# Cross attentions of a decoder block: context channels split 128 and 64, keys ahead of values

## The chip, the cores and the metric

The kernel runs on one core of a Trainium2 chip. A core has TensorE for matrix products (PE in the profile, PEld its weight loads), VectorE (DVE), ScalarE (ACT), GpSimd (POOL) and SyncE (SP), which here only issues transfers. Matmuls write to PSUM, which has eight banks of 512 float32 values per partition; the kernel's tiles `mm` and `one` are one bank, `sc` and `pair` two. The metric is the device time of one execution in microseconds, lower is better.

## The reference

Six sublayers in a row, each `x = layernorm(x + f(x))`, all float32, on `x` of 8 batches of 256 tokens of 256 channels: a gated convolution, a cross attention, a routed expert layer, a self attention with rotary position, a second cross attention, and a masked attention over all tokens. The two cross attentions have the same form and each its own weights:

```python
q = (x @ Wq).reshape(B, Nq, h, dh)          # h = 16 heads of dh = 64
k = (context @ Wk).reshape(B, Nk, h, dh)    # 77 context rows per batch, 192 channels
v = (context @ Wv).reshape(B, Nk, h, dh)
scores = jnp.einsum('bqhd,bkhd->bhqk', q, k) * scale
attn = jax.nn.softmax(scores, axis=-1)
out = jnp.einsum('bhqk,bkhd->bqhd', attn, v).reshape(B, Nq, h * dh)
return out @ Wo + bo
```

## The kernel before

The sublayers follow one another, and the end of each (its `tail`, a list of pieces) is issued inside the start of the next. In the convolution (`mamba`) the work goes by four stripes of 512 tokens. For a stripe, `state` and `steps` (L249) make products on TensorE; ScalarE takes the absolute value (L257), the exponential (L258) and then, in `gated`, the logarithm (L263); VectorE makes `y` of it (L265 to L273, the first of these reading the PSUM bank of `steps`). ScalarE holds one set of function tables at a time; a change of set shows as ACT_TABLE_LOAD. `outputs` (L282), a layer norm and `turn_out` (transposes at L88, a copy at L93) end a stripe.

In `cross`, the keys are never multiplied with queries directly. `keys(q, part)` (L427) makes the transposed keys of two batches for eight heads; `weighted_keys(q, g)` (L445) multiplies them with Wq into `M`, two heads side by side on the upper and lower 64 rows of the array; `scores(u)` (L464) multiplies tokens with `M`. The same is done for values: `values(c, g)` (L370) makes the transposed values of a chunk of 128 of the 616 context rows (five chunks, the last of 104), `weighted_values(c, g)` (L389) multiplies them with Wo, two heads side by side, into `U`, which goes to DRAM (L402) and comes back per batch as `Ub` (L411, L415). A unit `u` is eight heads of one batch; there are 16. In unit `u` the kernel issues `scores(u + 1)` with its softmax (maximum and subtraction on VectorE, L471 and L473; exponential on ScalarE, L477; sums on VectorE, division on GpSimd, L484), `outputs(u - 1)` (L509), then pieces of keys and values by two small tables (`more`, and a branch on `k`), then `turn(u)`, the transposes of the probabilities (L493). Copies out of PSUM go to ScalarE and VectorE in turn (`evac`, L74 and L76). The pieces needed before unit -1 are the list `first`; `places` says behind which of them each piece of the previous `tail` goes. Each engine works through its own queue in order.

The context has 192 channels, more than the 128 rows of the array. Before, they are two halves of 96 rows: 16 matmuls for eight pairs of heads. The weights come as 96 x 2 x 1024.

The second cross attention is followed by `signs.add`, whose chain over ScalarE, VectorE and GpSimd (L1284 to L1298) runs in its units. Its first pieces stand behind the last block of the rotary attention, whose norm is on GpSimd (L116), behind a power of 128x16 (L1272).

Of the kernel before, what the change touches and what calls it, by code (L numbers as in the profile page):

```python
# [10 lines left out]
F32 = mybir.dt.float32  # L11
# [7 lines left out]
P = 128  # L19
# [3 lines left out]
NCTX, DCTX = 77, 192  # L23
EPS = 1e-5
# [25 lines left out]
def decoder_kernel(ctx: ExitStack, tc: tile.TileContext, a: dict, out: bass.AP):  # L50
    nc = tc.nc
# [91 lines left out]
    def mamba(xs, W, cv, my, close):  # L143
# [4 lines left out]
        with pool_of(tc, name="m1", bufs=1) as m1, pool_of(  # L148
            tc, name="m2", bufs=2
        ) as m2, pool_of(tc, name="mps", bufs=2, space=PSUM) as mps:  # L150
            done, xc, sz, y, bc = [], {}, {}, {}, {}

# [5 lines left out]
            def one():  # L158
                return mps.tile([P, 512], F32, tag="one", name="one")
# [76 lines left out]
            def state_sums(s, bc_p):  # L236
                ps = one()
                last = nc.tensor.matmul(ps, ones[:16, :], bc_p[:16, :], start=True, stop=True)
                bc[s] = m1.tile([P, 512], F32, tag="bc", name="bc")
                nc.scalar.copy(bc[s], ps)  # L240
                return last
# [48 lines left out]
            def turn_out(s, half, ps):  # L290
                n_s, nT_s = done[s]
                transposed(ps, n_s[:, half * 2 : half * 2 + 2, :], nT_s, half)
# [3 lines left out]
            for s in range(4):  # L296
# [8 lines left out]
                if s > 1:  # L305
                    with tc.issue_after(last.ins):
                        for half in range(2):
                            turn_out(s - 2, half, one())
# [19 lines left out]
    def cross(xs, W, bias, ctxT, at_unit, after, tail):  # L328
# [10 lines left out]
        with ExitStack() as st:  # L339
# [7 lines left out]
            def mm():  # L347
                return cps.tile([P, 512], F32, tag="mm", name="mm")

            def pair():  # L350
                return cps.tile([P, 2, 512], F32, tag="sc", name="sc", bufs=3)
# [6 lines left out]
            def span(c):  # L358
                return c * P, min((c + 1) * P, NB * NCTX)

            def values(c, g):

                lo, hi = span(c)
                if g == 0:
                    VTs[c] = c1.tile([P, 8, P], F32, tag="VT", name="VT")
                ps = mm()
                for i in range(4):
                    hp = g * 4 + i
                    for kc in range(2):
                        nc.tensor.matmul(  # L370
                            ps[:, i * P : i * P + hi - lo], wv[:, kc, hp * P : (hp + 1) * P],
                            ctxT[:, kc, lo:hi], start=kc == 0, stop=kc == 1,
                        )
                evac(
                    VTs[c][:, g * 4 : g * 4 + 4, : hi - lo],
                    ps.rearrange("p (i n) -> p i n", i=4)[:, :, : hi - lo],
                )
# [41 lines left out]
            def keys(q, part):  # L419

                if part == 0:
                    KTs[q] = c1.tile([P, 8, 2 * NCTX], F32, tag="KT", name="KT")
                ps = pair()
                for i in range(4):
                    hp = part * 4 + i
                    for kc in range(2):
                        nc.tensor.matmul(  # L427
                            ps[:, i // 2, i % 2 * 2 * NCTX : (i % 2 + 1) * 2 * NCTX],
                            wk[:, kc, hp * P : (hp + 1) * P],
                            ctxT[:, kc, q * 2 * NCTX : (q + 1) * 2 * NCTX],  # L430
                            start=kc == 0, stop=kc == 1,
                        )
                nc.scalar.activation(
                    KTs[q][:, part * 4 : part * 4 + 4].rearrange("p (a i) n -> p a (i n)", a=2),
                    ps[:, :, : 4 * NCTX], AF.Copy, scale=0.125,
                )
# [93 lines left out]
            for c in range(NCH):  # L530
                for k in range(4):
                    u = (-2, -2, 1, 4, 8)[c] + k if c != 1 else -1 + k // 2
                    more.setdefault(u if c else -2, []).append(
                        lambda c=c, k=k: (values, weighted_values)[k // 2](c, k % 2)
                    )

            first = more[-2] + [
                lambda k=k: (keys, weighted_keys)[k // 2](0, k % 2) for k in range(4)
            ]
            places = (4, 5, 6, 7, 7, 8, 8)  # L540
# [12 lines left out]
            for u in range(-1, NU + 1):  # L553
# [9 lines left out]
                if 0 <= u and q + 1 < NB // 2:  # L563
                    if k < 2:
                        keys(q + 1, k)
                    else:
                        weighted_keys(q + 1, k - 2)
# [1011 lines left out]
    def cross_weights(pool, i, other=None):  # L1579
        return (  # L1580
            weight(pool, a[f"Wv{i}"], 2, 1024, 96), weight(pool, a[f"Wo{i}"], 8, D),
            weight(pool, a[f"Wk{i}"], 2, 1024, 96), weight(other or pool, a[f"Wq{i}T"], 8, D),
        )


    with ExitStack() as st:
# [4 lines left out]
        ctxT = const.tile([96, 2, NB * NCTX], F32, name="ctxT")  # L1591
# [8 lines left out]
        with pool_of(tc, name="wq", bufs=1) as wq:  # L1600
# [10 lines left out]
            nc.sync.dma_start(out=ctxT, in_=a["ctxT"].rearrange("(k p) n -> p k n", p=96))  # L1611
# [91 lines left out]
def _arrays(i):  # L1703

    def c(v):
        return np.ascontiguousarray(v)

    i = {k: np.asarray(v) for k, v in i.items()}
    consts, rot = _constants()
# [4 lines left out]
        "ctxT": c(i["ctx_768"].reshape(NB * NCTX, DCTX).T),  # L1714
# [8 lines left out]
        **{f"W{n}{l}": c(i[f"L{l}_xattn_W{n}"]) for n in "kvo" for l in (0, 1)},  # L1723
# [45 lines left out]
```

## Time and profile before

| what | value |
|---|---|
| three timed runs | 1440.02, 1442.06, 1445.01 us; median 1442.06 |
| profiled execution | 1440.51 us, its span 1438.7 us |
| TensorE clock granted, mean | 0.995 |
| busy: PE, DVE, ACT, POOL | 1369.4, 846.3, 652.0, 482.3 us |
| first cross attention on TensorE | from 159 to 416 us |
| second cross attention on TensorE | from 933 to 1191 us |

The page gives for each engine its busy time and the number of instructions. A group line has the code line, the engine, the operation, what is written and read, the shape (for a matmul, rows x columns of the weights, then rows x columns of the moving operand), the number of records, the busy time, the mean of one in ns, and the idle time before it with what ended it. A line of the chain of waits has the start, the length, the engine, the tile written, the code line and the number of records. A line of the waits has who waited, for whom, and the total, the number of times and the longest in us.

### The profile page before, as it was taken

What the parts mean: (1) busy time and instruction counts of PE and PEld (TensorE: products, weight loads), DVE (VectorE), ACT (ScalarE), POOL (GpSimd) and SP (SyncE); (2) the same over time, 40 slices, a digit from 0 to 9 for tenths busy, and PEclk for the clock granted to TensorE, in tenths of its full rate; (3) what the DMA queues carried; (4) which work ended last, traced back from release to release, by engine and by line L of the source; (5) the groups of instructions that cost most, each with busy time, mean ns of one, the idle gap of its engine ahead of it and who ended that gap; (6) DMA issues with size and microseconds to landing.
All of it is one profiled execution on the core that took longest, in us unless ns stands there. A gap on an engine that the chain in (4) does not pass through costs nothing.

```text
span 1438.7 us, 21959 instructions
## 1 busy us (share of the span) xinstructions
PE 1369.4 (95%) x7946; PEld 960.7 (67%) x7946; DVE 846.3 (59%) x2306; ACT 652.0 (45%) x1608; POOL 482.3 (34%) x509
## 2 busy tenths in 40 slices
PE   8999899999999999999989999999999999899996
PEld 3455578888866666656556666678878787566554
DVE  3776455465543323324668888745555663787885
ACT  3455433343331022221178787632342323877884
POOL 0100012122200133236336666332434445455541
PEclk9999999999999999999999999999999999999999
DMA  9000023333540022342120000024312210000100
GB/s 256 18 1 0 27 94 104 109 94 109 162 190 0 23 69 85 81 139 66 37 81 2 2 1 1 1 94 130 94 48 82 85 35 9 16 16 23 23 16 16
DMA packets 71679, 87.81 MB, mean 61 GB/s; under 512 B 5588, under 2 KB 66164, under 8 KB 71060
## 3 DMA queue, kind: packets, MB, share of 16 engines
q1 hardware_dynamic: 68164, 77.10, 17.6%
q0 software_dynamic: 3408, 9.31, 2.3%
q8 instruction: 64, 1.05, 0.3%
q14 instruction: 43, 0.35, 0.1%
HBM read 56.87 MB, written 29.52 MB: 60 GB/s over the span
## 4 chain that ended last, share of the span: by engine, by line
PE 78%; DVE 12%; POOL 3%; ACT 3%; issue 3%; DMA 0%; POOLq 0%; SPq 0%; DVEq 0%; ACTq 0%
PE mm L509 9%; PE sc L464 8%; PE mm L765 7%; DVE p L1018 6%; PE mm L828 5%; PE op L1055 4%; PE pair L249 4%; PE pair L178 4%; PE ps_sc L1040 4%; PE ps_sc L1009 4%; PE tr L782 3%; PE sc L427 2%; PE tr L842 2%; PE sc L445 2%; PE sc L493 2%
## 5 line engine op out<-in xcount | busy, mean ns | idle before, releaser
L1025 ACT ACTIVATE p<-p,nmx 128x256 f32<-128x256 f32 x512 | 252.9, 495 | 63.7 <-DVE nmx L1018 63.6
L484 POOL TENSOR_TENSOR p<-p,sm 128x616 f32<-128x616 f32 x60 | 72.6, 1215 | 247.3 <-DVE sm L481 217.0
L509 PE MATMUL mm<-Ub,pT 128*128 128x256 f32 (+1 forms) x640 | 144.6, 379 | 0.5 <-ACT pT L74 0.4
L464 PE MATMUL sc<-M,xT_s 128*128 128x308 f32 x512 | 139.6, 423 | 0.8 <-ACT pT L74 0.8
L1040 PE MATMUL ps_sc<-ident,p 128*128 128x128 f32 x1024 | 132.2, 276 | 7.6 <-DVE nmx L1018 3.7
L1040 PEld LDWEIGHTS ps_sc<-ident,p 128*128 128x128 f32 x1024 | 113.5, 141 | 34.4 <-issue 13.3
L509 PEld LDWEIGHTS mm<-Ub,pT 128*128 128x128 f32 (+1 forms) x640 | 120.8, 190 | 20.0 <-ACT pT L74 0.9
L765 PE MATMUL mm<-xT_s,w 128*128 128x512 f32 x256 | 114.9, 601 | 4.0 <-DVE h L771 3.2
L464 PEld LDWEIGHTS sc<-M,xT_s 128*128 128x128 f32 x512 | 94.0, 188 | 33.3 <-ACT pT L74 1.5
L477 ACT ACTIVATE p<-p 128x616 f32<-128x616 f32 x64 | 45.8, 716 | 149.9 <-DVE p L473 128.5
L1018 DVE CUSTOM_DVE_ANT_0 p<-ps_sc,term 128x256 f32<-128x256 f32 x256 | 90.7, 419 | 27.6 <-PE ps_sc L1009 27.5
L1018 DVE CUSTOM_DVE_ANT_0 p<-ps_sc,zero 128x256 f32<-128x256 f32 x256 | 90.7, 420 | 27.3 <-PE ps_sc L1009 25.7
L1025 ACT ACTIVATION_READ_ACCUMULATOR p<-p,nmx 128x1 f32 x512 | 95.8, 187 | 0.0
L765 PEld LDWEIGHTS mm<-xT_s,w 128*128 128x128 f32 x256 | 48.3, 192 | 59.0 <-issue 53.9
L802 POOL DMA_INDIRECT xb<-xd,token x39 | 37.2, 954 | 147.3 <-PE tr L809 81.1
L471 DVE TENSOR_REDUCE nmx<-sc 128x8 f32<-128x616 f32 x64 | 51.1, 798 | 54.3 <-PE sc L464 54.2
L1043 DVE COPY pT<-ps_sc 128x1024 f32<-128x1024 f32 x64 | 77.6, 1213 | 2.8 <-PE ps_sc L1040 2.8
L1043 ACT COPY pT<-ps_sc 128x1024 f32<-128x1024 f32 x64 | 63.7, 996 | 28.8 <-PE ps_sc L1040 28.7
L828 PE MATMUL mm<-wE,xbT 128*128 x156 | 73.5, 593 | 0.3 <-ACT xbT L814 0.3
L769 ACT ACTIVATE g<-mm 128x512 f32<-128x512 f32 x32 | 19.1, 597 | 104.3 <-PE mm L765 98.7
L113 POOL TENSOR_SCALAR rstd<-mv 128x2 f32<-128x2 f32 x48 | 10.7, 224 | 159.3 <-DVE mv L111 158.8
L480 DVE TENSOR_REDUCE sm<-p 128x8 f32<-128x616 f32 x64 | 50.5, 790 | 22.6 <-ACT p L477 21.9
(291 smaller groups left out, 2663.6 us busy)
## 6 DMA issues: line engine op xcount, KB each, us to landing
Ub<-ud SPq DMA_DIRECT2D x32, 512.0 KB
ud<-U SPq DMA_DIRECT2D x16, 616.0 KB
wE<-in_wE SPq DMA_DIRECT2D x4, 1536.0 KB
yd<-y SPq DMA_DIRECT2D x39, 128.0 KB
Ub<-ud SPq DMA_DIRECT2D x32, 104.0 KB
ud<-U SPq DMA_DIRECT2D x4, 608.0 KB
x_s<-in_x SPq DMA_DIRECT2D x8, 256.0 KB
w<-in_Wo SPq DMA_DIRECT2D x2, 1024.0 KB
```

What stands on the lines that cost most here:

```text
L178: last = nc.tensor.matmul(ps[:, i, :], w_in[:, kc, c * P : (c + 1) * P], xT_s[:, kc, :], start=kc == 0, stop=kc == 1,)
L249: last = nc.tensor.matmul(ps[:, i, :], w_dt[:, kc, c * P : (c + 1) * P], xc[s][kc // 2][:, kc % 2, :], start=kc == 0, stop=kc == 3,)
L464: nc.tensor.matmul(sc[:, a, : 4 * NCTX], xT_b[:, kc, j * P : (j + 1) * P], M[:, a * 4 : a * 4 + 4, kc, at : at + NCTX], start=kc == 0, sto ...
L484: engine.tensor_tensor(pv, pv, bcast(sm, 2, [P, 8, NCTX]), ALU.mult)
L509: nc.tensor.matmul(o[:, j * D : (j + 1) * D], pT[:n, c, j * P : (j + 1) * P],  Us[b][:n, g, c], start=g == 0 and j == 0 and c == 0, stop=g ...
L765: nc.tensor.matmul(ps, w[:, kc, cols], xT_s[:, kc, :], start=kc == 0, stop=kc == 1)
L828: nc.tensor.matmul(ps, xT[:, kc, :], column(j, kc * 512, 512), start=kc == 0, stop=kc == 1)
L1009: self.last_score = nc.tensor.matmul(scs[s // 2][:, s % 2, :], self.queries(b, c, s, qb), self.keys(b, c, s), start=True, stop=True, tile_ ...
L1018: self.last = nc.vector.tensor_tensor_reduce(out=p[:, h, :], in0=s4[:, h, :], in1=self.term(b, qb), scale=-1.0, scalar=3.0e38, op0=ALU.add ...
L1025: nc.scalar.activation(p[:, h, :], p[:, h, :], AF.Exp, bias=nmx[:, qb, n : n + 1], scale=-1.0, accum_out=sums[:, qb, n : n + 1],)
L1040: nc.tensor.transpose(tr[:, at : at + P], p[:, h, kb * P : (kb + 1) * P], ident)
L1043: (nc.scalar.copy if j else nc.vector.tensor_copy)(self.pT[b, c, j][:, :, :, qb * P : (qb + 1) * P], tr.rearrange("p (h k t) -> p h k t", ...
```

## The change

The context channels are split 128 and 64. The rest of 64 rows is put twice into `ctxT`, on partitions 0 to 63 and 64 to 127, and the rest of the weights is laid out with one pair of heads on the upper 64 partitions and the next on the lower ones. A new function `from_context` makes keys or values of all 16 heads at once: eight matmuls of 128 rows, then eight of 64 rows, two beside each other, each into its own bank of a pair. It uses the two-bank tiles for values too. The first pieces of `cross` have the order keys, values, weighted keys, weighted values. In the units, all keys of a quarter go into one unit, all values of a chunk into one, and the weighted values of chunks 2 to 4 move a unit earlier. In the convolution an exponential of one column is issued behind the copy of `bc`, and the two copies of `turn_out` in the last stripe go to VectorE.

```diff
+            warm = m1.tile([P, 1], F32, name="warm")
+            nc.gpsimd.memset(warm, 0.0)
...
-                nc.scalar.copy(bc[s], ps)
+                with tc.issue_after(nc.scalar.copy(bc[s], ps).ins):
+                    nc.scalar.activation(warm, warm, AF.Exp)
...
-                            turn_out(s - 2, half, one())
+                            turn_out(s - 2, half, one(), nc.vector.tensor_copy if s == 3 else None)
...
+            def from_context(w, lo, hi, copies, dst):
+                n, pss = hi - lo, [pair(), pair()]
+                for g in range(2):
+                    for a in range(2):
+                        for i in range(2):
+                            hp = g * 4 + a * 2 + i
+                            nc.tensor.matmul(
+                                pss[g][:, i, a * n : (a + 1) * n], w[:, 0, hp * P : (hp + 1) * P],
+                                ctxT[:, 0, lo:hi], start=a == 0, stop=False,
+                            )
+                for g in range(2):
+                    for a in range(2):
+                        for i in range(2):
+                            rest, k = DHEADS + (g * 2 + a) * P, slice(i * 64, (i + 1) * 64)
+                            nc.tensor.matmul(
+                                pss[g][:, i, a * n : (a + 1) * n], w[k, 0, rest : rest + P],
+                                ctxT[k, 1, lo:hi], start=False, stop=a == 1,
+                                tile_position=(i * 64, 0),
+                            )
+                    copies[g](
+                        dst[:, g * 4 : g * 4 + 4, :n].rearrange("p (a i) n -> p i a n", a=2),
+                        pss[g][:, :, : 2 * n].rearrange("p i (a n) -> p i a n", a=2),
+                    )
+            def values(c):
+                VT = VTs[c] = c1.tile([P, 8, P], F32, tag="VT", name="VT")
+                second = nc.scalar.copy if c == 0 else nc.vector.tensor_copy
+                from_context(wv, *span(c), (nc.scalar.copy, second), VT)
...
+            def keys(q):
+                KT = KTs[q] = c1.tile([P, 8, 2 * NCTX], F32, tag="KT", name="KT")
+                def scaled(dst, src):
+                    nc.scalar.activation(dst, src, AF.Copy, scale=0.125)
+                from_context(wk, q * 2 * NCTX, (q + 1) * 2 * NCTX, (scaled, scaled), KT)
...
-            for c in range(NCH):
-                for k in range(4):
-                    u = (-2, -2, 1, 4, 8)[c] + k if c != 1 else -1 + k // 2
-                    more.setdefault(u if c else -2, []).append(
-                        lambda c=c, k=k: (values, weighted_values)[k // 2](c, k % 2)
-                    )
-            first = more[-2] + [
-                lambda k=k: (keys, weighted_keys)[k // 2](0, k % 2) for k in range(4)
+            for c in range(1, NCH):
+                for k in range(3):
+                    u = (-1, 1, 4, 8)[c - 1] + (k if c > 1 else k // 2)
+                    more.setdefault(u, []).append(
+                        lambda c=c, k=k: weighted_values(c, k - 1) if k else values(c)
+                    )
+            first = [
+                lambda: keys(0), lambda: values(0),
+                lambda: weighted_keys(0, 0), lambda: weighted_keys(0, 1),
+                lambda: weighted_values(0, 0), lambda: weighted_values(0, 1),
             ]
-            places = (4, 5, 6, 7, 7, 8, 8)
+            places = (1, 1, 4, 5, 5, 6, 6)
...
-                    if k < 2:
-                        keys(q + 1, k)
-                    else:
+                    if k == 0:
+                        keys(q + 1)
+                    elif k > 1:
                         weighted_keys(q + 1, k - 2)
...
-            weight(pool, a[f"Wv{i}"], 2, 1024, 96), weight(pool, a[f"Wo{i}"], 8, D),
-            weight(pool, a[f"Wk{i}"], 2, 1024, 96), weight(other or pool, a[f"Wq{i}T"], 8, D),
+            weight(pool, a[f"Wv{i}"], 1, 1536), weight(pool, a[f"Wo{i}"], 8, D),
+            weight(pool, a[f"Wk{i}"], 1, 1536), weight(other or pool, a[f"Wq{i}T"], 8, D),
...
-        ctxT = const.tile([96, 2, NB * NCTX], F32, name="ctxT")
+        ctxT = const.tile([P, 2, NB * NCTX], F32, name="ctxT")
...
+    def two_rests(w):
+        rest = w[P:].reshape(DCTX - P, 4, 2, P).transpose(2, 0, 1, 3).reshape(P, 4 * P)
+        return c(np.concatenate([w[:P], rest], 1))
...
+        "ctxT": c(np.concatenate([ctxT, ctxT[P:]])),
```

## The prediction

> **What bounds the kernel now.** I read the page first, then the chain of waits in order of time over both cross attentions, then the groups by form, the waits by stage, and the timelines around the two starts.
>
> ```profile
> span 1438.7 us, 21959 instructions
> PE 1369.4 (95%) x7946; PEld 960.7 (67%) x7946; DVE 846.3 (59%) x2306; ACT 652.0 (45%) x1608; POOL 482.3 (34%) x509
> PE 78%; DVE 12%; POOL 3%; ACT 3%; issue 3%; DMA 0%; POOLq 0%; SPq 0%; DVEq 0%; ACTq 0%
> ```
>
> TensorE is busy 95% of the span and makes 78% of the chain that ended last. What matters is whether that holds where the edit works. In the chain of waits, a stretch of the first cross attention and a `weighted_keys` from another unit:
>
> ```profile
> 234.44 2.30 PE sc L445 x32
> ...
> 323.07 2.09 PE sc L427 x16
> 325.17 1.76 PE mm L370 x16
> 326.93 1.09 PE sc L493 x10
> 328.02 4.15 PE sc L464 x16
> ```
>
> Piece follows piece without a gap. From 200 to 392 us the waits of TensorE add up to 0.8 us. So a microsecond of keys (L427) or values (L370) is a microsecond of the end. A float32 matmul of the code makes two records, so x16 is eight matmuls. By form:
>
> ```profile
> L445 PE MATMUL sc<-KT,w 64*128 64x154 f32 x512 | 37.9, 298 | 0.0
> L427 PE MATMUL sc<-ctxT,w 96*128 96x154 f32 x256 | 36.3, 295 | 0.0
> L370 PE MATMUL mm<-ctxT,w 96*128 96x128 f32 x256 | 31.4, 278 | 2.4 <-ACT xT_s L93 2.4
> L370 PE MATMUL mm<-ctxT,w 96*128 96x104 f32 x64 | 7.7, 274 | 0.0
> ```
>
> L445 is the row to look at: 512 records with 64 rows cost as much as 256 of the same 154 columns with 96 rows (L427). Two half-array matmuls on different rows run side by side: 0.072 us a record against 0.131. And 104 columns of L370 cost what 128 cost (1.76 us per sixteen in the chain), so full-row records have a floor near 0.11 us whatever their columns.
>
> Only the starts have gaps: the waits of 155 to 200 us, then of 930 to 950 us.
>
> ```profile
> PE sc L389 <- DVE VT L76: 2.5, 1, 2.5
> PE mm L370 <- ACT xT_s L93: 2.4, 3, 0.9
> PE sc L389 <- ACT VT L74: 1.6, 1, 1.6
> ...
> PE sc L389 <- DVE VT L76: 2.8, 1, 2.8
> ```
>
> **Part 1: 128 and 64 rows in place of 96 and 96.** Keys of two batches were two groups of L427, 4.19 us. Now eight full-row matmuls (one such group, 2.10) and eight half-row ones, four pairs: half of L445's x32, 1.15. Where the array goes from full to half rows or back the chain shows about 0.1 us (L427 takes 2.19 before L389, 2.10 elsewhere; L370 takes 1.89 after L445 or L389, 1.77 elsewhere); I add 0.1, as before had some of these changes too. 3.35 us, 0.85 saved, eight times: 6.8 us.
>
> A chunk of values was 3.6 us (1.77 or 1.89, twice). Now 1.77 full-row, and eight half-row matmuls of 128 columns, which the trace does not have. Below: L445's rate scaled by columns, 1.15 x 128/154 = 0.95. Above: L445 unscaled, 1.15; far above, the full-row floor, 1.77, if the loads of a pair do not overlap. I take 1.0, as L445 has the same rows and weight shape. With the change 2.87, about 0.7 saved, ten times: 7.0 us. Part 1: 13.8 us, with 12 and 15 as near ends, and 6.1 if loads do not overlap.
>
> [...]
>
> **Part 2: keys first, in the first cross attention.** I walk the new order with old durations, on the old clock. TensorE ends the last transposes (L88) at 159.9. The first key matmul takes the banks of those transposes, whose copies the edit puts on VectorE behind `gated`, which ends at 160.97; two copies (0.6 each) free the banks at 162.25: a wait of 2.35, where L370 waited 0.7. Keys to 165.6. Values wait for the L265 that reads the last step's bank; it needs Ln. Here the table counts:
>
> ```profile
> 159.21 1.02 ACT L257 ACTIVATE e<-pair 128x1024 f32<-128x1024 f32 x1 [3.04 <-PE pair L249]
> 160.72 1.28 ACT L258 ACT_TABLE_LOAD   x1
> 164.86 1.06 ACT L263 ACTIVATE e<-e 128x1024 f32<-128x1024 f32 x1
> ```
>
> The load moves into the 3.04 us that ScalarE idles before L257, with one exponential of 128x1 (not in the trace; between the 0.19 of a 128x1 accumulator read and the 0.58 of a 128x512 copy). 1.9 us at most: covered. Were the cover gone, Ln would come that much later. With two copies (0.48, 0.06 on the path) moved to VectorE too, Ln ends near 163.7, L265 near 164.9: before the keys end. No wait. [...]
>
> Values to 168.5, two transposes, then both `weighted_keys` (4.6 us; eight copies of 0.6 us on ScalarE keep pace), first `weighted_values` 1.85, outputs 3.65, the second, outputs: scores start near 185, against 190.79. Chunk 1 follows with about 1 us of wait (its VT copy queues on ScalarE behind an exponential), and 0.1 later. Waits: 6.5 before (0.7, 0.8, 1.6, 2.5, 0.9), 3.4 after: 3.1 us gained.
>
> **Part 3: keys first, in the second.** No `gated` is in the way and weights are there; L370's 2.8 wait for VT goes. What is late next is the block from the rotary attention:
>
> ```profile
> 936.16 2.93 POOL L1272 TENSOR_TENSOR gss<-gss,nhalf 128x16 f32<-128x16 f32 x1
> 940.23 2.43 POOL L116 TENSOR_SCALAR x_s<-r,mv,rstd 128x256 f32<-128x256 f32 x2
> ```
>
> Its transposes (L88) moved from 946.06 to behind the values, at 940.0, but GpSimd delivers at 942.66, behind L1272. New wait: 2.7 us, with both `weighted_keys` queued behind it on TensorE. Another 0.6 for chunk 1's VT; gone are 2.8 and 0.7 (at 971). Net 0.2.
>
> **Moved at no cost.** `weighted_values` of chunk 0 now come last, so the way of U through DRAM starts later:
>
> ```profile
> 943.29 8.58 SPq L402 DMA_DIRECT2D ud<-U  x4
> 959.49 1.15 SPq L411 DMA_DIRECT2D Ub<-ud  x1
> ```
>
> By the stretches of DMA traffic it falls from 229 to 14 GB/s at 965: 21.7 us from the first issue. The new first issue is near 951, so both halves land by 972.7, and `outputs` 0 needs the first near 975: covered by scores, chunk 1 and keys, with 2 us to spare; in the first cross attention (first issue near 177, need near 210) 11 us. SyncE's queue keeps its order per chunk; the weights for the experts still stand behind the last readers of Wv, Wo and Wk. Later chunks run `weighted_values` a unit earlier, so their loads only gain. Keys and values now hold two pairs of banks: by the order of the changed program each new pair was read one group earlier (a 0.6 to 0.7 us copy against 1.0 of matmuls), so nothing in steady units; bound 0.5 us each. The POOL chain of the second cross attention that makes TensorE wait 1.8 and 1.6 us (behind L1298) starts at the same matmul and has the same work behind it: unchanged. In the convolution TensorE has no wait after 16 us, so warm exponentials there change nothing. ctxT grows by a third (462 to 616 KB), long before 159 us.
>
> **Sum.** 13.8 + 3.1 + 0.2 = 17.1; the walk itself gives 19 as early groups were slower than steady ones. I take 18. Against the profiled execution's 1440.5 us (span 1438.7 and 1.8 around it): 1422.5. The median of three runs stands 1.5 above that execution, so I forecast 1424.
>
> **Rivals.** Loads bound the half-row values (for it: the 0.11 floor at 104 columns; against it: L445): 10 x 0.77 lost, 1431. New waits: two pairs of three are held at once in every from_context; if each costs its bound of 0.5, 18 x 0.5 lost, 1433; against it, the waits are on copies that the timeline has done earlier. Slower: pairs neither overlap nor hide loads once they continue sums that a full-row matmul has begun, which nothing in this trace does. A half group then takes 16 x (0.11 + 0.12) = 3.7 us, 2.6 more than I count, 18 times: 47 lost, 1471. It decides from about 1 us extra a group; L445's start-and-stop pairs speak against it, not fully. The change doing nothing: half groups run one after the other at full-row price; then part 1 costs 2 us in array changes and 3.3 are gained at the starts: 1440.5.
>
> **How the numbers follow.** Forecast 0.64 (its own range 1418 to 1430); loads 0.12; waits 0.10; nothing 0.05; slower 0.05; better, 1413 (steady waits of before vanish too and the walk holds) 0.04. What a measurement can tell is about 0.3%, 4.3 us. Faster 0.90, same 0.05, slower 0.05. The range takes in loads and waits: 1415 to 1436, some 0.13 left out.
>
> **What would show it.** Right: sixteen half-row records in about 1.0 (values) and 1.15 us (keys); TensorE's first key matmul behind VectorE's xT copy near 162; scores at 185; a 2.7 us wait on POOL x_s near 940; no wait for Ub. Wrong: half groups above 1.7 us, or waits on KT or VT in every unit, or on Ub.

## The result and the profile after

| | before | after |
|---|---|---|
| timed runs | 1440.02 to 1445.34 us, median 1443.53 | 1423.13 to 1426.36 us, median 1424.32 |
| profiled execution, its span | 1440.51, 1438.7 us | 1423.73, 1421.9 us |

The ratio after to before is 0.9871 with a 95% interval of 0.9847 to 0.9896: 1.3% faster. The forecast was 1424.0 in a range of 1415 to 1436.

The page of the changed kernel, its span, busy times and the shares of the chain:

```profile
span 1421.9 us, 21978 instructions
PE 1358.5 (96%) x7946; PEld 947.0 (67%) x7946; DVE 847.1 (60%) x2306; ACT 651.6 (46%) x1612; POOL 483.3 (34%) x510
PE 65%; DVE 12%; POOL 3%; issue 2%; ACT 2%; DMA 1%; POOLq 0%; DVEq 0%; ACTq 0%; SPq 0%
```

TensorE has the same number of records and is busy 10.9 us less. It remains the bound. The shares of the chain add up to 85%, as the chain could be followed back only to 196 us; so TensorE's 65% is not to be held against the 78% before. Code lines have moved: keys and values are now both in `from_context`, L375 for the full-row matmuls and L384 for the half-row ones; `weighted_values` is L411, `weighted_keys` L457, `scores` L476, `turn` L505, `outputs` L521, the transposes L89.

The groups by form (busy us, mean ns) and a stretch of the chain in unit order:

```profile
L375 PE MATMUL sc<-ctxT,w 128*128 128x154 f32 x128 | 19.3, 307 | 2.2 <-DVE xT_s L94 2.2
L375 PE MATMUL sc<-ctxT,w 128*128 128x128 f32 x128 | 16.0, 278 | 0.0
L384 PE MATMUL sc<-ctxT,w 64*128 64x154 f32 x128 | 11.0, 312 | 0.0
L384 PE MATMUL sc<-ctxT,w 64*128 64x128 f32 x128 | 9.3, 285 | 0.0
```

```profile
259.10 2.10 PE sc L375 x16
261.19 1.25 PE sc L384 x16
262.44 1.98 PE sc L375 x16
264.42 1.09 PE sc L384 x16
265.51 1.24 PE sc L505 x10
```

Sixteen half-row records take 1.25 us in keys and 1.09 in values, sixteen full-row ones 2.10 and 1.98 (1.78 where no half-row group is just ahead). Nothing stands between the pieces.

The waits of TensorE in the stretches of 155 to 200, 915 to 940 and 940 to 1150 us:

```profile
PE sc L375 <- DVE xT_s L94: 2.2, 1, 2.2
PE sc L411 <- ACT VT L389: 0.8, 1, 0.8
...
PE mm L89 <- POOL x_s L117: 2.1, 2, 1.3
...
PE sc L505 <- DVE U L77: 3.4, 4, 1.1
PE sc L411 <- ACT VT L389: 0.6, 1, 0.6
```

The two foreseen waits are there, 2.2 us for VectorE's `xT` and 2.1 for GpSimd's `x_s`. So are the smaller two for `VT`. No wait for `Ub` appears.

To see where the 16.8 us of span went, cut TensorE's timeline at six points. "Falls" counts stretches of about 3.4 us in which the granted clock was 0.50 (more of them below; the one at the very end of each run is left out).

| stretch of TensorE | before | after | difference | predicted |
|---|---|---|---|---|
| start to the last transposes of the convolution | 159.0 | 159.4 | +0.4 | 0 |
| A: from there to scores(0) | 31.8 | 28.0 (1 fall) | -3.8 | -4.65 |
| B: to the experts' first matmul | 225.4 | 219.9 | -5.5 | -5.35 |
| C: to the second cross attention's first context matmul | 517.5 (1 fall) | 516.0 | -1.5 | 0 |
| D: to its scores(0) | 19.7 | 17.7 | -2.0 | -1.75 |
| E: to the last sublayer's first matmul | 231.9 | 226.5 | -5.4 | -5.35 |
| F: to the end | 253.4 (2 falls) | 254.4 (3 falls) | +1.0 | 0 |

The predicted column spreads the prediction's own terms: one batch pair of keys and one chunk of values (0.85 and 0.7) in A and in D, with 3.1 and 0.2 for the starts; three batch pairs and four chunks in B and in E.

E is less than it looks. In both kernels the last sublayer's TensorE waits for VectorE's `x_s` soon behind the cut between E and F, and this wait grew. Before, then after:

```profile
1185.27 3.69 PE L974 MATMUL ps_sc<-xT_s,w 128*128 128x256 f32 x16 [0.88 <-DVE r L103]
1191.29 1.22 PE L88 MATMUL ps_mm<-ident,x_s 128*128 128x128 f32 x4 [2.33 <-DVE x_s L116]
...
1167.52 3.62 PE L988 MATMUL ps_sc<-xT_s,w 128*128 128x256 f32 x16
1174.68 1.14 PE L89 MATMUL ps_mm<-ident,x_s 128*128 128x128 f32 x4 [3.54 <-DVE x_s L117]
```

From scores(0) to the end of that wait it is 237.95 us before and 233.65 after: 4.3 us less, not 5.4. The rest of F is 247.4 and 247.3, so the +1.0 of F is this wait, which stands at 3.5 us in every profile of the changed kernel and of its variants.

### The profile page after: what moved, and what is told of

Same layout as the page of the kernel before. It is cut to its first block, busy times and chain, and to the rows that moved or that the text cites. A ratio compares the mean times of both kernels' runs of the same rounds, so it can differ in the third digit from the quotient of the medians.

```text
span 1421.9 us, 21978 instructions
## 1 busy us (share of the span) xinstructions
PE 1358.5 (96%) x7946; PEld 947.0 (67%) x7946; DVE 847.1 (60%) x2306; ACT 651.6 (46%) x1612; POOL 483.3 (34%) x510
## 4 chain that ended last, share of the span: by engine, by line
PE 65%; DVE 12%; POOL 3%; issue 2%; ACT 2%; DMA 1%; POOLq 0%; DVEq 0%; ACTq 0%; SPq 0%
PE mm L521 9%; PE sc L476 8%; PE mm L779 7%; DVE p L1032 6%; PE mm L842 5%; PE op L1069 4%; PE ps_sc L1054 4%; PE ps_sc L1023 4%; PE tr L796 4%; PE tr L856 2%; PE sc L505 2%; PE sc L457 2%; PE sc L411 2%; PE sc L375 2%; PE ps_mm L988 1%
## 5 line engine op out<-in xcount | busy, mean ns | idle before, releaser
L521 PE MATMUL mm<-Ub,pT 128*128 128x256 f32 (+1 forms) x640 | 144.6, 379 | 0.5 <-ACT pT L75 0.4
L476 PE MATMUL sc<-M,xT_s 128*128 128x308 f32 x512 | 139.0, 423 | 1.1 <-ACT pT L75 1.1
L521 PEld LDWEIGHTS mm<-Ub,pT 128*128 128x128 f32 (+1 forms) x640 | 120.8, 190 | 20.0 <-ACT pT L75 0.9
L476 PEld LDWEIGHTS sc<-M,xT_s 128*128 128x128 f32 x512 | 94.4, 188 | 35.3 <-ACT pT L75 2.1
L1057 ACT COPY pT<-ps_sc 128x1024 f32<-128x1024 f32 x64 | 63.7, 996 | 26.8 <-PE ps_sc L1054 26.7
```

The lines of the kernel that those rows point to most:

```text
L476: nc.tensor.matmul(sc[:, a, : 4 * NCTX], xT_b[:, kc, j * P : (j + 1) * P], M[:, a * 4 : a * 4 + 4, kc, at : at + NCTX], start=kc == 0, sto ...
L521: nc.tensor.matmul(o[:, j * D : (j + 1) * D], pT[:n, c, j * P : (j + 1) * P],  Us[b][:n, g, c], start=g == 0 and j == 0 and c == 0, stop=g ...
L1057: (nc.scalar.copy if j else nc.vector.tensor_copy)(self.pT[b, c, j][:, :, :, qb * P : (qb + 1) * P], tr.rearrange("p (h k t) -> p h k t", ...
```

## Experiments

All times and ratios below stand beside runs of the kernel before on the same chip. For differences of a few us the timed medians are too coarse (their intervals are about 0.1 to 0.4% either way), so each verdict also goes by the same stretches of TensorE's timeline.

### 96 and 96 rows in the new order

```diff
-                            hp = g * 4 + a * 2 + i
-                            nc.tensor.matmul(pss[g][...], w[:, 0, ...], ctxT[:, 0, lo:hi], start=a == 0, stop=False)
...
+                            for kc in range(2):
+                                nc.tensor.matmul(pss[g][...], w[:, kc, ...], ctxT[:, kc, lo:hi], start=kc == 0, stop=kc == 1)
```

> The changed kernel with 96 and 96 channels again (sixteen matmuls of 96 rows for all heads), its order, tiles and starts kept. Theory (the rows carry the change, steady price): a half-row group measured 1.25 us (keys) and 1.09 us (values) in the changed kernel, a full-row one 2.1 and 1.77, so 8 x 0.85 + 10 x 0.68 = 13.6 us come back: profiled execution 1435.5 to 1438, ratio to the kernel before 0.996 to 0.998. Rival (order and starts carry it): 1424 to 1429.

Measured: 1433.49 us, ratio 0.9941 (0.9926 to 0.9957), span 1433.1 with 6 falls. The chain has keys and values of one unit as one piece:

```profile
261.82 7.76 PE sc L376 x64
```

7.76 is 4.19 for the keys and 3.57 for the values, against 3.35 and 3.07 in the chain of the changed kernel above. So the rows alone shorten a group of keys by 0.84 us and one of values by 0.5 (behind keys) or 0.7 (elsewhere). Over eight groups of keys and ten of values (six of them behind keys) that is 8 x 0.84 + 6 x 0.5 + 4 x 0.7 = 12.5 us, but the end moved by about 9. Stretches A, B, D and E are 29.3 (1 fall), 223.9, 17.7 and 229.9, so against the changed kernel the rows bring 1.2, 4.0, 0 and 3.4, together 8.6. In D they bring nothing: TensorE waits for the rotary attention's last block in both, 0.9 us with 96 rows and 2.1 with 128 and 64. The waits for `VT` (0.8 in the first cross attention, 0.6 in the second) are not there with 96 rows, and those for `U` are 2.8 instead of 3.4. The new waits add up to 3.2 us: this is what faster groups gave back.

The other side is as telling: with 96 rows, the rest of the edit alone gives 1.5 us in B, 2.0 in D and 2.0 in E against the kernel before, and 2.5 in A in spite of a fall. That is waits, not work. With the idle times of over 0.1 us ahead of TensorE's matmuls as waits and the rest of a stretch as work (us):

| stretch | before: waits, work | 96 rows: waits, work | changed: waits, work |
|---|---|---|---|
| A | 5.6, 26.1 | 2.2, 27.1 (1 fall) | 2.3, 24.5 (second profile, no fall) |
| B | 3.0, 222.4 | 1.6, 222.3 | 2.3, 217.6 |
| D | 2.8, 16.9 | 0.9, 16.8 | 2.1, 15.5 |
| E | 5.2, 226.7 | 3.1, 226.7 | 4.4, 222.1 |

Gone with 96 rows are, in B, 0.9 us for `xT` ahead of chunk 1 and 0.8 for VectorE's `r` at the experts' first matmul (against 0.3 more for the copies `pT`); in E, 0.7 of `weighted_values` for `U`, 0.5 of `turn` for `U`, and the 0.9 for `r` that the longer wait for `x_s` takes back. A chunk of values in one piece is 3.57 against 1.78 and 1.98, but the work of B and E as a whole is the same as before. Which part of the edit (the two-bank tiles, the order of the pieces) takes which wait away was not tested.

### Rows with the old starts

```diff
-                lambda: keys(0), lambda: values(0),
-                lambda: weighted_keys(0, 0), lambda: weighted_keys(0, 1),
-                lambda: weighted_values(0, 0), lambda: weighted_values(0, 1),
+                lambda: values(0),
+                lambda: weighted_values(0, 0), lambda: weighted_values(0, 1),
+                lambda: keys(0), lambda: weighted_keys(0, 0), lambda: weighted_keys(0, 1),
...
-            places = (1, 1, 4, 5, 5, 6, 6)
+            places = (3, 3, 4, 5, 5, 6, 6)
...
-                with tc.issue_after(nc.scalar.copy(bc[s], ps).ins):
-                    nc.scalar.activation(warm, warm, AF.Exp)
+                nc.scalar.copy(bc[s], ps)
...
-                            turn_out(s - 2, half, one(), nc.vector.tensor_copy if s == 3 else None)
+                            turn_out(s - 2, half, one())
```

> The 128/64 rows alone: first pieces as values, weighted values, keys, weighted keys, no warm exponential, the last stripe's copies on ScalarE; the rest as changed. Theory (parts add up as predicted): 3.1 us lost in the first cross attention, 0.2 in the second, 1427 us. My own amendment: the values now take two-bank tiles, the first of which lies on the banks of the last transposes, so that the first value matmul waits for ScalarE's second copy behind the table load, until 163.5 us, 3 us of idle; scores(0) near 191, the whole 1427 to 1430. Rival (the starts are worth nothing): 1424, scores(0) near 187.5.

Measured: 1424.53 us, ratio 0.9882 (0.9844 to 0.9920), span 1423.0 with 5 falls: the changed kernel's time, as the rival had it and neither of my two sums. The wait that the amendment foresaw is there, on TensorE's timeline of this kernel (start, length, in brackets the idle time before):

```profile
163.89 3.30 PE L372 MATMUL sc<-ctxT,w 128*128 128x128 f32 x16 [3.56 <-ACT xT_s L94]
```

Stretches A, B, D and E are 29.7 (1 fall), 219.9, 16.9 and 225.8. If the fall cost 1.7 us, the most that one takes, A is 28.0 against 26.8 in the changed kernel without a fall (below): the new start is worth 1.2 us in the first cross attention (1.6 if it cost the 1.25 by which the changed kernel's two profiles differ in A). In the second it costs 0.8 in D and 0.7 in E. So keys ahead of values, the early table and the copies on VectorE were worth next to nothing in sum. The old waits for `VT`, 2.5 and 2.8 us, were gone here although the order was the old one. That left a suspect: with the edit both copies of chunk 0's values go to ScalarE.

### Old starts and the old copies

```diff
-                second = nc.scalar.copy if c == 0 else nc.vector.tensor_copy
-                from_context(wv, *span(c), (nc.scalar.copy, second), VT)
+                from_context(wv, *span(c), (nc.scalar.copy, nc.vector.tensor_copy), VT)
```

> The rows alone with the old starts, and chunk 0's second copy of values back on VectorE as in the kernel before. Theory A (the copy engine, not the order, took the old waits of 2.5 and 2.8 us for VT away): in the first cross attention weighted values wait for VectorE's VT until its gated step ends near 169.5 us, scores(0) 1.0 to 2.0 us later than with the copy on ScalarE (28.0 us from the last transposes' start without the clock's fall): 29 to 30; in the second the wait of 2.8 comes back in part, 1 to 2.8 us. Theory B (the order did it): both starts as with the copy on ScalarE, 28.0 and 16.9 us.

Measured: 1426.36 us, ratio 0.9894 (0.9872 to 0.9916). The waits of TensorE from 155 to 187 us and then from 905 to 940 us:

```profile
PE sc L407 <- DVE VT L386: 1.2, 1, 1.2
...
PE sc L407 <- DVE VT L386: 1.2, 1, 1.2
```

A is 31.1 (1 fall) against 29.7 (1 fall) with the copy on ScalarE, D 17.5 against 16.9. The copy engine is worth 1.4 and 0.6 us, inside what theory A said for A and below its 1 us for D; theory B falls. What still separates this kernel from the one before, 2.2 us in D and some 2.4 in A (with 1.7 taken for the fall), is the rows, the groups in one piece and the two-bank tiles together.

### Without the early table

```diff
-                with tc.issue_after(nc.scalar.copy(bc[s], ps).ins):
-                    nc.scalar.activation(warm, warm, AF.Exp)
+                nc.scalar.copy(bc[s], ps)
```

> The changed kernel without the exponential that loads the table ahead. Theory (as predicted: what it saves is covered, here the more so as the first keys took 5.2 us): the logarithm of the last stripe ends 1.3 us later, VectorE's read of the steps' bank near 166.6 us, and the first value matmul came at 167.8: TensorE's scores(0) stay at 187.4 to 187.6, 1424 us. Rival (the load is on the path): scores(0) 1.3 us later, 1425.

Measured: 1429.47 us, ratio 0.9906 (0.9874 to 0.9938). The profile has eight falls of the clock, all behind 680 us, where the edit changes nothing; so the time says nothing of it. TensorE's timeline does:

```profile
163.65 2.36 PE L372 MATMUL sc<-ctxT,w 128*128 128x154 f32 x16 [2.19 <-DVE xT_s L94]
165.94 1.32 PE L381 MATMUL sc<-ctxT,w 64*128 64x154 f32 x16
167.70 1.16 PE L372 MATMUL sc<-ctxT,w 128*128 128x128 f32 x8 [0.44 <-DVE y L267]
169.74 1.16 PE L372 MATMUL sc<-ctxT,w 128*128 128x128 f32 x8 [0.88 <-ACT KT L443]
```

No fall came between the keys and the values this time, the keys were done early, and the values then waited 0.44 us for VectorE's read of the steps' bank and 0.88 for the copy of the keys, which ScalarE had behind the late logarithm. (In the changed kernel a table load of 1.28 us stands at the early exponential, at 156.58 us, and the step's exponential at 160.66 has none ahead of it; in the kernel before it had one of 1.28 us, at 160.72.) A is 28.1 without a fall, 1.3 more than 26.8. My expectation rested on the slow keys of one profile and missed; the early table is worth 1.3 us, about all of the 1.2 to 1.6 that the new start has over the old one in A.

### The same rows after one another

```diff
-                    for a in range(2):
-                        for i in range(2):
+                    for i in (g, 1 - g):
+                        for a in range(2):
                             rest, k = DHEADS + (g * 2 + a) * P, slice(i * 64, (i + 1) * 64)
```

> The changed kernel, the half-row matmuls ordered so that two of the same rows follow each other: 2 of 7 neighbours differ in rows, against 7 of 7. Theory (two neighbours on different rows run side by side, on the same rows one after the other at the full-row price of 0.131 us a record of 154 columns and 0.11 of 128): 5/7 of the saving is lost, 0.6 us a keys group and 0.5 us a values group, 8 x 0.6 + 10 x 0.5 = 9.8 us: 1433 us; sixteen half-row records in 1.85 and 1.6 us. Rival 1 (64 rows are cheaper by themselves): unchanged, 1424. Rival 2 (loads of the same rows do not overlap with matmuls at all): 0.23 us a record, groups of 3 us, 1450 or more.

Measured: 1427.31 us, ratio 0.9900 (0.9861 to 0.9940), span 1425.7 with 6 falls. The chain:

```profile
257.82 2.10 PE sc L375 x16
259.91 1.36 PE sc L384 x16
261.28 1.98 PE sc L375 x16
263.26 1.21 PE sc L384 x16
```

1.36 and 1.21 us, 0.11 and 0.12 more than with strict change of rows; B grows by 0.7 and E by 0.5. My theory asked for 1.85 and 1.6 and falls. I took it to mean that 64 rows are cheap by themselves, and tried that with no change of rows at all.

### All half-row matmuls on rows 0 to 63

```diff
-                            rest, k = DHEADS + (g * 2 + a) * P, slice(i * 64, (i + 1) * 64)
+                            rest, k = DHEADS + (g * 2 + a) * P, slice(0, 64)
...
-                                tile_position=(i * 64, 0),
+                                tile_position=(0, 0),
```

> The changed kernel with all half-row matmuls on rows 0 to 63: the pairs of heads that belong on rows 64 to 127 get the first rows' weights and context, so half of the rests are wrong; count and shapes of the instructions are the same, and no two neighbours lie on different rows. Theory as it stands after the reordering (sixteen same-rows-mostly records took 1.36 and 1.21 us against 1.25 and 1.09; 2 of 7 neighbours differed): the remaining two changes are worth as much as the five did at most, so 1.45 and 1.3 us, 18 groups x 0.2 = 3.6 us more than the changed kernel: 1428; 64 rows are cheap by themselves. Rival (it is the change of rows that makes them cheap, and two changes in seven were enough to keep most of it): full-row prices, 2.1 and 1.8 us, 18 x 0.75 = 13 us more: 1437.

Measured: 1437.69 us, ratio 0.9978 (0.9968 to 0.9988): most of the gain is gone. The chain:

```profile
261.71 2.10 PE sc L375 x16
263.80 2.29 PE sc L384 x16
266.09 1.98 PE sc L375 x16
268.07 1.98 PE sc L384 x16
```

Half rows cost what full rows cost: 2.29 and 1.98 us, where the full-row groups ahead of them take 2.10 and 1.98. The rival was right and the theory of cheap rows falls: the gain is two matmuls on different rows side by side, 1.25 and 1.09 us with the rows in turn. What the reordering shows beside it is that they need not alternate one by one: in the sequence 0 0 1 1 1 1 0 0 most of the overlap survives. How far apart they may be is open. The 18 groups are 8 x 1.04 + 10 x 0.89 = 17.2 us longer, of which A, B, D and E show 1.5, 5.8, 0 and 5.3; here too waits give way (that for `x_s` falls from 2.1 to 0.3 us, those for `VT` vanish).

A record on one row group takes 0.143 us in the keys and 0.124 in the values, against 0.078 and 0.068 with the rows in turn. The reordered kernel's 1.21 us is more overlap than neighbours of different rows alone would give: with 5 of 7 neighbours at the price of one row group I estimate 1.09 + 5/7 x (1.98 - 1.09) = 1.7 us from the measured prices.

### Filling, or shortening, the first wait

Work that nobody reads, in TensorE's wait:

```diff
                 n, pss = hi - lo, [pair(), pair()]
+                if tail and w is wk and lo == 0:
+                    filler = mm()
+                    for _ in range(2):
+                        nc.tensor.matmul(filler, ident, ctxT[:, 0, :512], start=True, stop=True)
```

> The changed kernel with two matmuls of 128x512 into a bank that nobody reads (0.93 us each by the convolution's rows) in TensorE's wait of 2.2 us ahead of the first keys; nothing else moves. Theory (the idle time lowers the granted clock: it showed 0.91, 0.50, 0.74 in the 6 us behind the wait): the clock stays at 1.00, the first keys take 3.4 us instead of 5.2, scores(0) near 185.7, the whole 1.8 us less, 1422. Rival (the clock falls there for another reason, or work that follows takes it back): scores(0) at 187.4, 1424.

Measured: 1424.06 us, ratio 0.9882 (0.9861 to 0.9904); A is 26.8 with no fall. The condition holds in the second cross attention too, where the filler adds 2.0 us ahead of the keys; there the 2.1 us wait for `x_s` is gone and scores(0) come only 0.4 us later from the start of the rotary attention on. As the changed kernel's second profile shows (below), A is 26.8 without a filler when no fall comes, so this run alone does not say that the filler kept the clock up.

The copies of the last transposes ahead of the gated product:

```diff
-                return nc.vector.tensor_tensor(t, t, sz[s][c2], ALU.mult)
+                with tc.issue_after(behind.ins) if behind else nullcontext():
+                    return nc.vector.tensor_tensor(t, t, sz[s][c2], ALU.mult)
...
-                gated(s, 0, *e0)
+                gated(s, 0, *e0, turned if s == 3 else None)
```

> The changed kernel with VectorE's two copies of the last transposes ahead of the last product of the gated step instead of behind it. Theory: TensorE's wait falls from 2.2 to 1.0 us (first keys from 161.4 us); if the clock falls by the length of the idle time it stays at 1.00, the keys end at 164.8, the values wait for VectorE's read of the steps' bank until 165.4, scores(0) near 185.1, 2.4 us less, 1421.5. Rival (the clock falls all the same): keys end near 166.5, scores(0) near 186.2. Rival (the wait moves to the steps' bank, whose read comes later as VectorE is held up): 187.4.

Measured: 1425.50 us, ratio 0.9891 (0.9869 to 0.9912). TensorE's timeline:

```profile
162.10 2.36 PE L378 MATMUL sc<-ctxT,w 128*128 128x154 f32 x16 [0.94 <-DVE xT_s L94]
164.39 1.32 PE L387 MATMUL sc<-ctxT,w 64*128 64x154 f32 x16
166.11 1.16 PE L378 MATMUL sc<-ctxT,w 128*128 128x128 f32 x8 [0.40 <-DVE y L270]
168.15 1.16 PE L378 MATMUL sc<-ctxT,w 128*128 128x128 f32 x8 [0.88 <-ACT KT L449]
```

The wait fell from 2.19 to 0.94 us, and 0.40 and 0.88 took its place at the values. A is 26.8: nothing gained. The second rival holds: the wait moved.

### The same two kernels once more

> The changed kernel, unaltered, one more profile. Theory (the falls of the granted clock to 0.5 come at a phase of their own and only meet TensorE's gaps by chance): the fall near 164 us need not be there, others may appear at 680, 720 or 935 us, each worth up to 1.7 us; from the start of the last transposes to scores(0) 26.3 to 26.8 us without a fall and 28.0 with one; everything else within 0.3 us. Rival (a gap of 2.2 us always brings it): the fall at 164 us again, 28.0.

Measured: 1424.18 us, span 1422.4. TensorE's clock in the windows of the first profile of the changed kernel (the third figure from the right is the granted clock), and the start of the keys in the second profile:

```profile
162.00:164.00 2.00, 1.37 (x9) 1.38 (x10) 0.57 (x1) 1.99 (x2) 0.00 (x0) 0.91 0.03 8
164.00:166.00 2.00, 2.00 (x9) 1.79 (x7) 1.85 (x2) 0.09 (x1) 0.00 (x0) 0.50 0.00 0
166.00:168.00 2.00, 2.00 (x18) 1.73 (x18) 1.96 (x3) 0.61 (x2) 0.00 (x0) 0.74 0.00 0
```

```profile
162.34 2.36 PE L375 MATMUL sc<-ctxT,w 128*128 128x154 f32 x16 [2.19 <-DVE xT_s L94]
164.63 1.32 PE L384 MATMUL sc<-ctxT,w 64*128 64x154 f32 x16
165.88 2.42 PE L375 MATMUL sc<-ctxT,w 128*128 128x128 f32 x16
```

The wait is the same 2.19 us, but the second time the clock stayed at 1.00 and the keys took 3.5 us instead of 5.2. A is 26.8, B 219.9, D 17.7, E 226.5: apart from the fall these stretches repeat. Falls appear at 679 and 717 us instead, where the first profile had none. The theory holds.

> The kernel before, unaltered, one more profile. Theory as for the changed kernel: stretches without a fall of the clock repeat within 0.3 us (31.8 us from the last transposes to scores(0), 225.4 to the experts' start, 231.9 for the second cross attention), and the falls lie elsewhere or differ in number. Rival: the same falls at 690, 1192 and 1236 us.

Measured: 1442.51 us, span 1440.7. A, B and E repeat to 0.1 us (31.8, 225.4, 231.9). Falls that the first profile had at 689, 1191 and 1235 us lie at 689, 1194 and 1232 (two in a row there); two more in a row fall at 938 and make D 22.4 instead of 19.7. So the places are partly the same, their number is not.

### The last block's transposes later in the second cross attention

```diff
-            places = (1, 1, 4, 5, 5, 6, 6)
+            places = (1, 1, 4, 5, 5, 6, 6) if len(tail) > 1 else (3,)
```

> The changed kernel with the transposes of the rotary attention's last block behind both weighted keys in the second cross attention. Theory: the 2.1 us of wait for GpSimd's x_s at 931 to 932.4 us go, as the block is there by then; scores(0) of the second cross attention 2.1 us earlier (939.0) and the end too, 1421.6. Rival (a later wait takes it back, the one for the last block's x_s at 1170 us or for VectorE's U): scores(0) earlier, the end as it was, 1424.

Measured: 1421.10 us, ratio 0.9860 (0.9839 to 0.9881), span 1417.4. TensorE's timeline of this kernel:

```profile
928.88 4.62 PE L457 MATMUL sc<-KT,w 64*128 64x154 f32 x64
933.43 0.66 PE L89 MATMUL mm<-ident,x_s 128*128 128x128 f32 x4
934.01 3.72 PE L411 MATMUL sc<-w,VT 64*128 64x256 f32 x32
937.67 4.42 PE L476 MATMUL sc<-M,xT_s 128*128 128x308 f32 x16
```

The transposes follow the weighted keys with no wait. D is 15.2 against 17.7, E is the same 226.5, and the wait for `x_s` behind it the same 3.5, so no later wait takes the 2.5 us back.

### Together

The copies first, the late transposes, and the two transposes of stripe 2 between the first keys and the first values:

```diff
-            places = (1, 1, 4, 5, 5, 6, 6)
+            places = (0, 0, 4, 5, 5, 6, 6) if len(tail) > 1 else (3,)
```

> Copies first and late transposes together, and the two transposes of stripe 2 between the first keys and the first values, where they fill the wait for the steps' bank. Theory (they add): 2.4 + 1.0 + 2.1 = 5.5 us less than the changed kernel, 1418.3; ratio to the kernel before near 0.983. Rival (waits follow one another, half is kept): 1421.

Measured: 1419.51 us, ratio 0.9849 (0.9829 to 0.9869), span 1416.4 with one fall. TensorE's timeline at the first start:

```profile
164.16 1.32 PE L387 MATMUL sc<-ctxT,w 64*128 64x154 f32 x16
165.40 1.09 PE L89 MATMUL mm<-ident,x_s 128*128 128x128 f32 x8
166.33 1.06 PE L378 MATMUL sc<-ctxT,w 128*128 128x128 f32 x8
167.91 1.16 PE L378 MATMUL sc<-ctxT,w 128*128 128x128 f32 x8 [0.52 <-ACT KT L449]
```

The moved transposes cover the wait for the steps' bank; 0.52 us for the keys' copy is left. A is 25.6 and D 15.2: by the stretches 1.2 and 2.5, 3.7 us less than the changed kernel without a fall, not the 5.5 that adding the parts gave, as 2.4 of these counted a fall and a wait that moved. The intervals of the timed ratios overlap with that of the changed kernel, so the stretches carry this verdict.

## Why the prediction was right, and where it was not

**Part 1, the prices.** Keys: 3.35 predicted, 2.10 + 1.25 measured. Half-row values: 1.0 predicted, 1.09 measured; L445's rate was the right neighbour, and the kernel with one row group shows the far bound as real (1.98). Where values follow keys the change of rows costs 0.2 us, not 0.1, so a chunk there took 3.07 instead of 2.87. The chain before had this price already: L370 takes 1.98 there behind L445 or L389, against 1.78, where I had read 1.89, and L427 takes 2.09 or 2.10 ahead of L389 too, where I had read 2.19. The price step held within some 0.2 us a group.

**Part 1, the sum.** By the table under the run with 96 rows, TensorE's work fell by 1.6, 4.8, 1.3 and 4.6 us in A, B, D and E, together 12.3, where the sum had 13.8. The step that failed is that every microsecond of keys and values is a microsecond of the end. With the rest of the edit in place the rows brought 8.6 us in the stretches: 3.2 us came back as waits for `x_s`, `VT` and `U` that are not there, or shorter, with slower groups. Most of these waits I had, as prices of the order in parts 2 and 3 (2.7 for `x_s`, about 1 and 0.6 for `VT`; measured 2.1, 0.8 and 0.6); what I had wrong is that the parts add up, each with a worth of its own.

**What made up for it.** Waits that I had not looked at: those for VectorE's `r`, 0.8 us at the experts' first matmul and 0.9 at the last sublayer's. The forecast of B and E (5.35 each) was met by 5.5 and 5.4 with other parts than I had named, 4.8 and 4.6 of work and 0.7 and 0.8 of waits, and 1.1 of E came back in F. That the whole came within 0.3 us of 1424.0 is in part luck.

**Part 2.** The wait of 2.35 us was measured as 2.19. Scores(0) came at 187.4 and 185.9 us in the two profiles, near 185 as forecast only in the one without the fall, where A is 5.0 shorter (predicted 4.65). But the reason was only partly right. Its first step, that the order takes the old waits away, fails: the old order with the new groups and copies loses just 1.2 to 1.6 us in A, and putting one copy back on VectorE costs 1.4. The early table is as covered as I had it, and worth 1.3 us: the values do wait for the logarithm when it is late.

**Part 3.** The wait behind GpSimd's power is there, 2.1 us instead of 2.7, and D moved by 2.0 against 1.75, though 1.55 of that was to come from the rows, which bring nothing there with the rest of the edit in place. Its net of 0.2 for the order was too kind: old starts are 0.8 us shorter in D, and moving only the transposes gains 2.5.

**Moved at no cost.** No wait for `Ub` in either cross attention: right. The waits for VectorE's `U`, 3.4 us in sum, are now four instead of two, the same sum: right. The waits for VectorE's `r` are gone in every kernel with values in two-bank tiles. That the tiles are the reason was not tested.

**Rivals.** Loads that bound the half-row values (1431) and pairs that do not overlap (1471) are excluded by 1.09 and 1.25 us. No run shows the 0.11 + 0.12 us a record of the second; the dearest half-row records, all on one row group, took 0.143 us. New waits of 0.5 us in every group are not there: in B and E no matmul of keys or values waits at all. Half groups at full-row price with nothing gained is what the kernel with one row group shows: 1437.7 against that rival's 1440.5. The one mechanism for slower, no overlap once sums continue, does not exist here: the pairs continue sums and overlap as L445 does, 0.078 us a record in the keys against its 0.072.

## What to carry to other kernels

Here a contraction of 192 rows was better cut as 128 and 64 than as 96 and 96, 3.35 us against 4.19 for a group of keys, with two of the 64-row halves on different rows of the array; with all of them on the same rows the half group alone rose from 1.25 to 2.29 us. Look for a line in the profile that already pairs half arrays and take its rate: L445's 0.072 us a record, with 0.1 for the change of rows, made 1.25 us a half group of keys, and 1.25 was measured. Where TensorE gets faster, ask at each start and each slow neighbour engine what is next late: here a quarter of the rows' gain turned into waits, and 2.5 us were to be had by moving four transposes behind work that was ready. A part's worth is shown by leaving it out, not by the wait that vanished with it: the order got the credit for what a copy on another engine did, and a wait of 0.9 us that vanished came back as a longer one a few us later.

## What the runs showed that I had not expected

In these profiles the granted clock of TensorE falls to 0.50 for about 3.4 us at a time, each fall costing up to 1.7 us (in the windows above: 0.09 + 0.50 + 0.26 of 2 us each). The fourteen profiles of this study had between one and eight of them ahead of the last one, at places that differ between two profiles of the same kernel. A part of what the timed runs scatter goes with this: of the runs with one row group, the slowest (1441.0 us) had a mean granted clock of 0.988, the fastest (1435.97) one of 0.994. At the first start, with a wait of 3.6 us ahead of the keys or values a fall came in 2 of 2 profiles, with 2.2 us in 2 of 7, with under 1 us in 0 of 5.

The places are not chance alone. In the clock records of each profile all falls begin whole multiples of 3.413 us apart: in the first of the changed kernel they begin 1010.35 and 40.96 us apart, 296 and 12 times that. With the first profiles of the two kernels cut by that grid into cells of 3.413 us (each from 20 us after its start to 14 us ahead of its end), all 4 cells in which TensorE's matmuls left more than 2.0 us idle were followed by a fall in the next cell. Of the cells that were not in a fall themselves, 2 of 19 with 1.0 to 2.0 us idle were, and none of 787 with less. In the other twelve profiles, of the cells that TensorE's busy time in windows of 2 us places surely, it was 10 of 10, 5 of 48 and 1 of 4214. So it matters where a wait lies on the grid: the wait of 2.2 us at the first start lay whole in one cell in one profile (a fall); in the other six the cell held 1.3 to 1.8 us of idle time (one fall). The wait of 2.5 us in the kernel before was cut into cells with 1.4 to 1.5 us of it or of smaller waits, and no fall came in either profile. What decides between 1 and 2 us is open.

For a reader of profiles this means that two kernels are to be compared by stretches without a fall: A of the changed kernel was 28.0 us with one and 26.8 without.
